# A convolution in transformed blocks: blocks of 4 rows by 2 columns in place of 4 rows, for images 1 to 3

## The chip, the cores and the metric

The kernel runs on one core of a Trainium2 chip. The metric is the time of one execution on the device in microseconds, as the median of several runs. Before the change it is 2772.66 us (three runs, 2771.19 to 2774.41). The core's engines are TensorE (PE), VectorE (DVE), ScalarE (ACT) and GpSimd (POOL); SyncE (SP) issues most DMAs. Each engine takes its instructions in the order in which the program gives them.

## The reference

Four images x of 256 channels and 48 x 48 pixels, all in fp32. Two layers, each added to its input:

```python
x = x + _L0_conv_ref(_gn(x), ...)   # layer 0: 3x3 convolution, batch norm, relu, qkv, attention, projection
x = x + _L1_conv_ref(_gn(x), ...)   # layer 1: dynamic filters, 1x1 convolution, batch norm over the batch

def _L0_conv_ref(Vx, ...):
    x = lax.conv_general_dilated(Vx, conv_w, window_strides=(1, 1), padding='SAME', ...)  # 256 -> 256, 3x3
    x = relu(batch_norm(x + conv_b))          # stored mean and variance
    qkv = einsum('oc,bchw->bohw', qkv_w, x) + qkv_b        # 8 heads of 32
    attn = softmax(einsum('bhdn,bhdm->bhnm', q, k) * scale)
    out = einsum('oc,bchw->bohw', proj_w, einsum('bhem,bhnm->bhen', v, attn)) + proj_b

def _L1_conv_ref(x, W_cat, W_scale, ...):
    guidance = _conv(x, W_cat, pad=1)         # 45 maps: 9 weights for each of 5 dilations
    outs = [x]
    for i, d in enumerate((1, 6, 12, 24, 36)):
        w = softmax(guidance[:, 9 * i:9 * (i + 1)], axis=1)
        outs.append(_dyn_branch(x, w, d))     # 9 shifted copies of x, weighted per pixel
    y = _conv(concatenate(outs), W_scale, pad=0)           # 1x1, then batch norm
```

`_gn` is a group norm with 32 groups. The change concerns the 3x3 convolution of layer 0 alone.

## The kernel before

The 256 channels stand as two halves (`h`) of 128 partitions. An image's 2304 pixels are handled in 6 chunks of 384 (`CH`). The order of all instructions is fixed when the program is built: the kernel keeps a table of estimated engine times (`clock`), and its planner `drive` gives PE the next step that is due by it.

The stages follow each other as start, attention 0, filters 0, attention 1, filters 1, attention 2, filters 2, attention 3, filters 3 with the end. The start stage makes the convolution of image 0 and its qkv alone. The filter stage of image b (`dynamic_filters`, layer 1 of image b) has the convolution and qkv of image b + 1 as filler (`other`): where no step of the filters is due, `drive` takes the next step of the filler. The last filter stage has no such filler.

A filter stage begins with the last projection (`pp`, L1120), the group norm of layer 1 (`pm_n` L662, `pv_n` L672, then the normalisation of `pad` at L636 and L1661) and the guidance product `pg` (L1197) of the first chunks. `far` gathers the dilated filters (matmuls L1395), `near` the filter of dilation 1 (products on DVE at L1461, sums on POOL at L1466), and `mixes` the final 1x1 product `py` (L1561).

The convolution (`conv`) transforms rows only: four output rows come from six input rows (`d`), through six row points `i` in the order `ORDER = (1, 2, 3, 4, 0, 5)`. `inputs` forms the six transformed inputs `v[i]` in three steps, on ACT and on DVE for image 0, on ACT and POOL for the others. For each point, each of two groups of rows `g` and each output half `o`, PE multiplies with six weight tiles (two channel halves by three columns `kx`) of 288 columns into one PSUM tile:

```python
pc = psum_tile(f"pc_{b}_{i}_{g}_{o}")
for h in range(NH):
    for kx in range(3):
        nc.tensor.matmul(m, u[:, h, kx, o * P : (o + 1) * P],
                         halves[g][:, h, i, :, kx : kx + WW], ...)
```

The tiles come from a pool of two buffers (`ps_c`). `outputs` reads each: points 1 and 3 are copied by ACT (`m`, L843), points 2 and 4 give sums and differences on DVE (L846 to L851), points 0 and 5 close four rows of the result (L827, L832, L856) and a relu on ACT (L814) writes `hid`. Then qkv follows: `pq` (L930) for q and k and `pv` (L951) for v. `hid` uses the same buffer as attention's output `ao`.

The transformed weights `u` are made once, in the start stage, by `Made`, and stored to DRAM as `u_d` (L762), six tiles of 768 KB. The filter stages load them back, one tile per row point (`taken`, L725), into a pool of two buffers. In the start stage POOL also issues the loads of all weights, twelve small stores (L1824), the mask copies (L596, L601), and the loads of the other images for their statistics (`xst`, L1692; DVE reads them at L650).

Of the kernel before, what the change touches and what calls it, by code (L numbers as in the profile page):

```python
# [16 lines left out]
N = HH * WW  # L17
# [40 lines left out]
def conv_preact_kernel(  # L58
# [483 lines left out]
    u_d = tc.dram_tile([6, P, NH, 3, C], F32, name="u_d")  # L542
# [3 lines left out]
    with tc.tile_pool(name="w", bufs=1) as wpool, tc.tile_pool(  # L546
        name="act", bufs=1
    ) as act, tc.tile_pool(name="u", bufs=2) as upool, tc.manual_schedule():
# [12 lines left out]
        wqkv = wpool.tile([P, NH, 3, C], F32, tag="wqkv", name="wqkv")  # L561
        wp = wpool.tile([P, NH, C], F32, tag="wp", name="wp")
# [53 lines left out]
        bn_s6 = wpool.tile([P, NH], F32, tag="bn_s6", name="bn_s6")  # L616


        pads = []
        for j in range(2):  # L620
            t = act.tile([P, NH, PADW * PADW], F32, tag=f"pad{j}", name=f"pad{j}")
            t = t.rearrange("p h (r w) -> p h r w", w=PADW)
            nc.gpsimd.memset(t[:, :, 0, :], 0.0)
            nc.gpsimd.memset(t[:, :, PADW - 1, :], 0.0)
            nc.gpsimd.memset(t[:, :, 1 : PADW - 1, 0], 0.0)
            nc.gpsimd.memset(t[:, :, 1 : PADW - 1, PADW - 1], 0.0)
            pads.append(t)
# [94 lines left out]
        def taken(i):  # L722

            u = upool.tile([P, NH, 3, C], F32, tag="u", name=f"u_{i}")
            nc.sync.dma_start(out=u, in_=u_d[i])  # L725
            return u

        class Made:


            def __init__(self, wc, pool):
                self.w = [wc[:, :, 3 * j : 3 * j + 3, :] for j in range(3)]
                self.u = {}
                self.pool = pool

# [10 lines left out]
            def home(self, i):  # L746
                return upool.tile([P, NH, 3, C], F32, tag="u", name=f"u_{i}")
# [4 lines left out]
            def __call__(self, i):  # L752
# [9 lines left out]
                nc.sync.dma_start(out=u_d[i], in_=u[i])  # L762
# [149 lines left out]

        def conv_qkv(b, gn, psum_tile, weights, ready, pool, between=()):

            hid = keep("h", f"hid_{b}")
            yield from conv(b, gn, psum_tile, weights, ready, pool, hid, between)
# [6 lines left out]
            for c in range(NCK):  # L923
                cols = slice(c * CH, (c + 1) * CH)
                for g in range(NH):
                    for s, dst, bias in ((0, q, Q_B), (1, k_, K_B)):
# [18 lines left out]
                        )  # L945
                        yield 2 * MM
# [31 lines left out]
        def attention(b, q, k_, vT, pools, spare, project, scratch):  # L978
# [132 lines left out]
            weigh(*steps[-1], prev)  # L1111
            close(last)
            return ao, chunk
# [25 lines left out]
        def dynamic_filters(b, ao, chunk, norm, other, pools):  # L1139
# [485 lines left out]
            def drive(streams):  # L1625

                due = [next(s, None) for s in streams]
                while any(d is not None for d in due):
# [9 lines left out]
                    else:  # L1638
                        got = next(other, None)
                        if got is not None:  # L1640
                            spent[0] += got
                        elif soonest < NEVER:
                            clock.t["PE"] = soonest

            if alone:
                other = late()

# [144 lines left out]
        u_next = None  # L1792
        norms = {}
# [269 lines left out]
```

## Time and profile before

| | |
|---|---|
| median of three runs | 2772.66 us |
| the profiled execution: time, span | 2766.55 us, 2764.8 us |
| mean granted TensorE clock | 0.99 |
| busy: PE, DVE, ACT, POOL | 95%, 73%, 64%, 23% |
| start stage | 0 to 147.9 us |
| filter stages 0, 1, 2 | 304.2, 303.8, 278.1 us long |
| attention stages | 365 to 370 us each |

How to read it: a line of the profile names the source line, the engine, the operation, output and inputs by the program's names, and the shapes. An fp32 matmul of the program appears as two records on PE. "Idle before" is the time in which the engine did nothing before the instruction, and behind the arrow stands what released it. Times within the trace count from the start of the span.

### The profile page before, as it was taken

To read this page: it belongs to the slowest core of one execution; us is meant where nothing else is said; L and a number is where in the kernel's file an instruction comes from. 1 tells how busy PE (TensorE), PEld (TensorE's weight loads), DVE (VectorE), ACT (ScalarE), POOL (GpSimd) and SP (SyncE) were. 2 spreads that over 40 slices of the span, in tenths; PEclk is the share of its full clock that TensorE was granted. 3 is DMA by queue.
4 is the path that set the end of the run, shared out by engine and by line. 5 is a ranking of instruction groups with operands and counts; after the bars stand their busy time and mean duration, and the time that the engine had idled before them with its cause. 6 is when DMAs were issued, how large, how long until landed. Compare 5 with 4: busy or idle time off the path is not lost. (4 is left out here: it accounts for less than half of the span.)

```text
span 2764.8 us, 42248 instructions
## 1 busy us (share of the span) xinstructions
PE 2638.8 (95%) x17108; PEld 1135.8 (41%) x17108; DVE 2025.3 (73%) x1956; ACT 1761.1 (64%) x2153; POOL 632.3 (23%) x583
## 2 busy tenths in 40 slices
PE   7999999899999999989999999999999999999994
PEld 5632223455662222345565222245566222234452
DVE  6578888656539888856644988894664988885476
ACT  3488988633349888843336889882335988873244
POOL 5100100435400100054430001006542001000352
PEclk9999999999999999999999999999999999999997
DMA  5604544223422444423360345442335244432465
GB/s 216 156 24 103 109 98 104 58 77 90 104 56 58 101 102 97 109 57 75 84 132 9 81 98 112 101 87 56 93 92 150 55 96 95 101 87 68 118 181 182
DMA packets 132522, 267.35 MB, mean 97 GB/s; under 512 B 55656, under 2 KB 97552, under 8 KB 131424
## 3 DMA queue, kind: packets, MB, share of 16 engines
q0 software_dynamic: 25952, 135.74, 21.6%
q1 hardware_dynamic: 106368, 128.84, 17.7%
q8 instruction: 136, 2.23, 0.3%
q14 instruction: 66, 0.54, 0.1%
HBM read 107.40 MB, written 34.46 MB: 51 GB/s over the span
## 5 line engine op out<-in xcount | busy, mean ns | idle before, releaser
L1050 DVE TENSOR_TENSOR acc<-acc,p 128x2048 f32<-128x2048 f32 (+1 forms) x572 | 1061.1, 1855 | 115.6 <-ACT p L1014 64.9
L1014 ACT ACTIVATE p<-se 128x1536 f32<-128x1536 f32 x648 | 938.7, 1449 | 0.1
L1005 PE MATMUL so<-q,k 32*128 32x512 f32 (+1 forms) x1440 | 726.4, 592 | 13.5 <-ACT p L1013 12.7
L1005 PE MATMUL se<-q,k 32*128 32x512 f32 (+1 forms) x4320 | 735.1, 592 | 0.0
L1034 PE MATMUL num<-p,vT 128*32 128x512 f32 (+1 forms) x5760 | 705.1, 560 | 4.6 <-ACT p L1014 2.4
L1013 ACT ACTIVATE p<-so 128x512 f32<-128x512 f32 x648 | 388.4, 599 | 186.8 <-PE se L1005 80.0
L1466 POOL TENSOR_TENSOR near<-near,prod 128x768 f32<-128x768 f32 x192 | 348.8, 1817 | 431.4 <-DVE prod L1461 424.7
L1005 PEld LDWEIGHTS so<-q,k 32*128 32x128 f32 x1440 | 216.1, 183 | 529.0 <-ACT p L1013 489.8
L1034 PEld LDWEIGHTS num<-p,vT 128*32 128x32 f32 x5760 | 133.8, 108 | 478.8 <-issue 444.3
L1054 POOL DMA_DIRECT2D scratch<-p x124 | 105.5, 851 | 772.3 <-ACT p L1014 519.8
L1461 DVE TENSOR_TENSOR prod<-wb,pad 128x768 f32<-128x768 f32 x192 | 181.9, 953 | 87.6 <-ACT wb L1448 75.6
L1561 PE MATMUL py<-far,wsc 128*128 128x384 f32 x704 | 236.7, 488 | 0.0
L1005 PEld LDWEIGHTS se<-q,k 32*128 32x128 f32 x4320 | 226.7, 183 | 5.4 <-ACT p L1014 4.1
L1448 ACT COPY wb<-ws 128x384 f32<-128x384 f32 x216 | 108.7, 507 | 171.3 <-DVE prod L1461 137.6
L1170 ACT COPY far<-far 128x512 f32<-128x512 f32 x82 | 87.9, 1099 | 137.4 <-PE far L1395 134.6
L1052 POOL DMA_DIRECT2D scratch<-p x32 | 17.9, 559 | 669.7 <-ACT p L1014 508.3
L1561 PEld LDWEIGHTS py<-far,wsc 128*128 128x128 f32 x704 | 131.1, 190 | 87.3 <-issue 1.8
L897 PE MATMUL pc<-cv_q,u 128*128 128x288 f32 x576 | 151.8, 415 | 8.2 <-DVE cv_q L788 6.2
L1197 PE MATMUL pg<-pad,wcat 128*45 128x384 f32 x864 | 149.1, 493 | 10.0 <-ACT lg L1255 4.4
L897 PE MATMUL pc<-cv_k,u 128*128 128x288 f32 x576 | 153.3, 410 | 4.3 <-DVE yt L832 2.7
L930 PE MATMUL pq<-hid,wqkv 128*128 128x384 f32 x384 | 125.6, 487 | 1.7 <-DVE yt L832 0.6
L897 PEld LDWEIGHTS pc<-cv_q,u 128*128 128x128 f32 x576 | 108.7, 192 | 43.2 <-DVE cv_q L788 6.3
(252 smaller groups left out, 2368.3 us busy)
## 6 DMA issues: line engine op xcount, KB each, us to landing
scratch<-p POOLq DMA_DIRECT2D x156, 768.0 KB, 5.7
ws<-w_d SPq DMA_DIRECT2D x216, 192.0 KB
pad<-in_x SPq DMA_DIRECT2D x14, 1152.0 KB
u<-u_d SPq DMA_DIRECT2D x18, 768.0 KB
xst<-in_x POOLq DMA_DIRECT2D x36, 192.0 KB, 6.9
x_d<-pad SPq DMA_DIRECT2D x36, 192.0 KB
y_d<-y SPq DMA_DIRECT2D x14, 384.0 KB
u_d<-u SPq DMA_DIRECT2D x6, 768.0 KB
```

The source lines that it names most:

```text
L897: nc.tensor.matmul(m, u[:, h, kx, o * P : (o + 1) * P], halves[g][:, h, i, :, kx : kx + WW], start=(h == 0 and kx == 0), stop=(h == NH - 1 ...
L930: nc.tensor.matmul(pq[:, :CH], wqkv[:, i, s, g * P : (g + 1) * P], hid[:, i, cols], start=(i == 0), stop=(i == NH - 1),)
L1005: nc.tensor.matmul(dst[:, at : at + n], k_[r, g, m * P : (m + 1) * P], q[r, g, q0 : q0 + n], start=True, stop=True,)
L1013: nc.scalar.activation(p[:, 0, :], s1, AF.Exp, scale=QS)
L1014: nc.scalar.activation(p[:, 1:, :], s3, AF.Exp, scale=QS)
L1034: nc.tensor.matmul(st["num"][r, at : at + n], vT[:, m, g * P + j * D : g * P + (j + 1) * D], p[:, j, at : at + n], start=(m == 0 and not s ...
L1050: nc.vector.tensor_tensor(st["acc"][:, js], other[:, js], p[:, js], ALU.add)
L1197: nc.tensor.matmul(pg[64 * s : 64 * s + NG, :CH], wcat[:, ii, k, :], shifted(ii, cc, k // 3 - 1, k % 3 - 1), start=(i == 0 and k == 0), st ...
L1448: nc.scalar.copy(pw[:, :CH], fetched[c, k][0])
L1461: nc.vector.tensor_tensor(prod.rearrange("p h (r w) -> p h r w", w=WW), wb, src, ALU.mult)
L1466: nc.gpsimd.tensor_tensor(cat, cat, prod, ALU.add)
L1561: nc.tensor.matmul(py[c][:, o, :CH], wsc[:, n * NH + i, o * P : (o + 1) * P], rhs, start=(n == 0 and i == 0), stop=(n == order[-1] and i = ...
```

## The change

For images 1 to 3 the convolution is also transformed along the columns: two output columns come from four input columns through four column products. The row transformation stays. Image 0 keeps the old `conv`.

- `Blocks` holds the transformed inputs. `stage0` to `stage3` form the row points from `gn` (1200 elements each), on ACT, DVE and POOL; `stage0` and `stage1` are placed at the end of the attention before, around its last `close`; `stage2` follows the first product of the first tile and `stage3` that of the third. `along(i)` makes the four column inputs of point `i` (576 elements each) on DVE or POOL, into what was v, `hid` or the pad.
- `conv_blocks` makes for each point `i`, each output half `o` and each column product `j` a PSUM tile with two matmuls of 288 columns. Products 1 and 2 are copied by ACT (`one`), summed and subtracted (`both`, `one`) on DVE or POOL, and then joined with products 0 and 3 into the point's output, which goes through the old row sums on 576 elements and a relu.
- The weights are stored in the start stage as column sets (`four`), one per point and output half, 512 KB each, made by ACT and POOL; the filter stages load twelve of them into thirds of one tile `ring`, which replaces the pool of two.
- The filler gives a time from which it can go on (`need`), and `drive` leaves it aside until then.
- Before a pad is loaded again, POOL clears its border (`clear`), as the pad now serves as a buffer.

```diff
-    u_d = tc.dram_tile([6, P, NH, 3, C], F32, name="u_d")
+    u_d = tc.dram_tile([6, NH, P, NH * 4 * P], F32, name="u_d")
...
+        TILES = [(i, o) for i in ORDER for o in range(NH)]
...
+        def taken(t):
+            i, o = TILES[t]
+            at = 1024 * ((t + 2) % 3)
+            u = ring[:, at : at + 1024]
+            nc.sync.dma_start(out=u, in_=u_d[i, o])
+            return u.rearrange("p (h j c) -> p h j c", h=NH, j=4)
...
-                nc.sync.dma_start(out=u_d[i], in_=u[i])
+                for o in range(NH):
+                    four = self.pool.tile([P, NH, 4, P], F32, tag="four", name=f"four_{i}_{o}", bufs=1)
+                    of = u[i][:, :, :, o * P : (o + 1) * P]
+                    nc.scalar.mul(four[:, :, 0], of[:, :, 0], 2.0)
+                    nc.scalar.mul(four[:, :, 3], of[:, :, 2], 2.0)
+                    tt = nc.gpsimd.tensor_tensor
+                    tt(four[:, :, 1], of[:, :, 0], of[:, :, 2], ALU.add)
+                    tt(four[:, :, 2], four[:, :, 1], of[:, :, 1], ALU.subtract)
+                    tt(four[:, :, 1], four[:, :, 1], of[:, :, 1], ALU.add)
+                    nc.sync.dma_start(out=u_d[i, o], in_=four.rearrange("p h j c -> p (h j c)"))
...
+            def stage0(self):
+                v, d = self.v, self.d
+                nc.scalar.mul(v[5], d[1], 4.0)
+                self.axpy(v[0], d[2], -4.0, d[4])
+                nc.gpsimd.tensor_tensor(v[5], d[3], v[5], ALU.subtract)
+            def stage1(self):
+                v = self.v
+                nc.vector.tensor_tensor(v[1], v[0], v[5], ALU.add)
+                self.along(1, nc.vector)
+                nc.gpsimd.tensor_tensor(v[2], v[0], v[5], ALU.subtract)
+            def stage2(self):
+                v, d = self.v, self.d
+                nc.gpsimd.tensor_tensor(v[3], d[4], d[2], ALU.subtract)
+                nc.gpsimd.tensor_tensor(v[6], d[3], d[1], ALU.subtract)
+                self.axpy(v[4], v[6], -2.0, v[3])
+                self.axpy(v[3], v[6], 2.0, v[3])
+            def stage3(self):
+                v, d = self.v, self.d
+                nc.gpsimd.tensor_tensor(v[0], v[0], d[2], ALU.subtract)
+                nc.gpsimd.tensor_tensor(v[5], d[5], v[5], ALU.subtract)
+                self.axpy(v[0], d[0], 4.0, v[0])
+                self.axpy(v[5], d[3], -4.0, v[5])
...
+            blocks.along(2)
+            for t, (i, o) in enumerate(TILES):
+                u = us.pop(t)
+                y = target(i, o).rearrange("p (n s) -> p n s", s=2)
+                parts = []
+                for n, j in enumerate((1, 2, 0, 3)):
+                    m = psum_tile(f"pc_{b}_{i}_{o}_{j}")[:, :XN]
...
+                    for h in range(NH):
+                        nc.tensor.matmul(m, u[:, h, j], z[:, h], start=(h == 0), stop=(h == NH - 1))
+                        clock("PE", MM * XN / CH)
+                        if h == 0:
+                            if n == 0:
+                                if t + 2 < len(TILES):
+                                    us[t + 2] = taken(t + 2)
+                                if o == 0:
+                                    if i == ORDER[0]:
+                                        blocks.stage2()
+                                    elif i == ORDER[1]:
+                                        blocks.along(ORDER[2])
+                                        blocks.stage3()
...
+                    if n < 2:
+                        one = pool.tile([P, XN], F32, tag="one", ..., bufs=4)
+                        nc.scalar.copy(one, m)
+                        parts.append(one)
+                        if n == 1:
+                            both = pool.tile([P, XN], F32, tag="both", ...)
+                            either(both, *parts, ALU.add, end)
+                            either(parts[0], *parts, ALU.subtract, end)
+                            parts[1] = both
...
             weigh(*steps[-1], prev)
+            following[0]()
             close(last)
+            following[1]()
...
-                        got = next(other, None)
-                        if got is not None:
-                            spent[0] += got
-                        elif soonest < NEVER:
-                            clock.t["PE"] = soonest
+                        open_at = need[0]()
+                        if open_at <= clock.t["PE"]:
+                            got = next(other, None)
+                            if got is not None:
+                                spent[0] += got
+                                continue
+                            need[0] = lambda: NEVER
+                        soonest = min(soonest, open_at)
+                        if soonest < NEVER:
+                            clock.t["PE"] = max(soonest, clock.t["PE"])
```

`either` gives an operation to DVE or POOL by the estimated clock; `axpy` is DVE's x * a + y, issued per channel half on the inputs, and not entered in the clock there.

## The prediction

> **What bounds the kernel now.** First the page's busy times, then the windows of each stage, then the timeline at the two places where the change puts new work in front of TensorE.
>
> ```profile
> PE 2638.8 (95%) x17108; PEld 1135.8 (41%) x17108; DVE 2025.3 (73%) x1956; ACT 1761.1 (64%) x2153; POOL 632.3 (23%) x583
> ```
>
> TensorE (PE) is the bound. The windows show where the convolution stands (columns: window, length, busy time and instructions of PE, PEld, DVE, ACT, POOL, granted clock, DMA share, GB/s):
>
> ```profile
> 0.00:147.90 147.90, 126.09 (x491) 93.19 (x491) 88.69 (x186) 57.65 (x100) 49.81 (x148) 1.00 0.57 174
> 513.20:817.40 304.20, 293.85 (x1306) 180.25 (x1306) 161.40 (x238) 109.60 (x185) 123.43 (x76) 0.99 0.33 78
> 1187.80:1491.60 303.80, 293.12 (x1306) 180.05 (x1306) 160.95 (x238) 109.72 (x185) 123.47 (x76) 0.99 0.32 78
> 1857.90:2136.00 278.10, 263.82 (x1211) 161.91 (x1211) 163.69 (x234) 107.06 (x183) 123.75 (x76) 0.99 0.36 97
> ```
>
> The first row is the start stage (convolution of image 0 alone), the others are the three filter stages: dynamic filters of one image, with convolution and qkv of the next as filler. PE is busy for 293 of 304 us there; DVE and POOL have room on average. What their queues do at the beginning of a stage decides this change, so the timeline of the start stage (start, duration, engine, line, what, idle before and its releaser):
>
> ```profile
> 19.65 8.91 PE L897 MATMUL pc<-cv_q,u 128*128 128x288 f32 x24 [6.22 <-DVE cv_q L788]
> 24.07 2.55 POOL L1824 DMA_DIRECT2D w_d<-e  x5 [4.32 <-DMA wsc<-in_scale_w]
> 29.98 6.09 PE L897 MATMUL pc<-cv_k,u 128*128 128x288 f32 x24 [1.41 <-ACT m L843]
> ```
>
> PE starts at 19.65 on ACT's and DVE's input sums; POOL is held by its DMA issues until 26.62; the third block of products waits for ACT's copy `m`. And of the second filter stage:
>
> ```profile
> 1196.26 4.46 PE L1120 MATMUL pp<-ao,wp 128*128 128x384 f32 x8 [2.75 <-DVE ao L1087]
> 1205.42 0.28 PE L662 MATMUL pm_n<-mvn,gmat 128*128 128x2 f32 x2
> 1211.54 2.17 PE L1197 MATMUL pg<-pad,wcat 128*45 128x384 f32 x12 [1.41 <-DVE pad L636]
> ```
>
> The norm's matmul `pm_n` stands in PE's queue at 1205.42, the first guidance product `pg` at 1211.54: everything of the filters comes after these two.
>
> **The sum's base.** The profiled execution took 2766.55 us (span 2764.8); the median of the runs is 2772.66, 6.1 above it. I sum against 2766.55 and add 6.1.
>
> **Products removed.** Per image, 6 row points x 4 blocks x 6 products = 144 become 6 x 2 x 4 x 2 = 96, all of 288 columns. In the start stage, blocks of 12 products (24 records) begin 5.82 us apart (53.84, 59.66, 65.47 on PE's timeline): 0.485 each. 48 x 0.485 = 23.3 us an image, 69.8 for three. As PE is 96% busy there, all of it would count if PE still had work at every moment.
>
> **New weights, start stage.** Each of the 6 weight sets is now turned into four columns twice (`four`, per output half): two ACT multiplications, three POOL adds of 256 elements, one 512 KB store. `four` has one buffer, so the next half's first ACT multiplication waits for the store to land, and in ACT's queue behind it stand the input sums, the `m` copies and the relus. Prices: POOL adds of 600 and 768 elements took 1.45 and 1.82 us, by that line 0.7 for 256, so 2.1 for three; ACT's 288-element copy took 0.40, so 0.7 for two. A store: the 768 KB `u_d` store issued at 50.80 kept the DMA engines busy at 0.93 from 51.6 to 53.7, 2.9 us; scaled, 2.6 for 512 KB. The other end is 5.7 us, the median to landing of the 768 KB `scratch` issue.
>
> - First product: POOL free 26.6, adds 28.7, store 31.4, ACT's second half 32.1, then cv_q multiplication 0.7 and DVE 2.4: PE starts at 35.2 instead of 19.65, +15.5.
> - Third block: DVE's weight sum ends 6.9 after PE's start (as at 26.51 now), 42.1; ACT's `wc` 1.5, two multiplications and POOL's adds together, store: 46.9; second half, table load, `m` copy: 49.7 instead of 29.98, +19.7 in all.
> - Point 3: POOL's mask copies (26.95 to 43.5 now, 16.6 us) follow the adds and end near 65.6. Then three rounds of adds and store (4.8 each) and 1.1 of ACT stand before the `m` copy: 81.1, where PE needs it at 53.84 + 19.7 = 73.5. +27.3 in all.
> - POOL's `xst` loads queue behind `four` adds, and DVE's statistics on them stand before DVE's reads of PSUM: about 3 more (0 to 6).
> - TensorE's clock: new idle times of 5 to 8 us, 2.5 (below).
>
> Sum +33. Bounds: +20 if the mask copies run at the short copies' 0.4 us for three (no wait at point 3) and `xst` costs nothing; +48 with stores of 5.7.
>
> **Start of each filter stage.** The order of the new instructions: POOL forms `v2` before the stage; then `along(2)` writes four 576-element tiles into `hid`, the buffer of `ao`, so it waits for `pp` to be read (about 1201.4, since the input work of stage0 delays DVE's `ao` by 0.6). POOL: 4 x 1.4 = 5.6, then two subtractions of 1200 elements (stage2), 2.75 each by the line of 600 and 768: 1212.5. On DVE, four `axpy` of 600 (0.78 each, as DVE's 600-element sums of image 0) wait for these, and behind them stands the norm's aggregate: 1212.5 + 3.1 + 0.9 = 1216.5. PE's `pm_n`, now at 1205.42, waits until then, +11.2, and the filler products behind it in PE's queue too. Before `pg`, two products of the second tile need ACT copies that stand behind ACT's 2.3 us normalisation: +2 more. On to the first far product (1241 now) I follow the queues to 1261, with 10 more products (4.9 us) done by then: a net stall of 15 us a stage, 45 in all. None of the planner's clocks counts these stage operations, so its order does not avoid it. Bounds: 8 a stage if POOL takes half the time for these, 18 if strided reads slow POOL by a fifth.
>
> **The rest of a filter stage.** DVE's 40 output operations of 288 (18 us) and some copies of far tiles go; about 19 + 4 of 576 (0.72), 24 + 6 of 288 (0.44), 10 of 600 and one of 1200 come: +23 of 161. ACT gains 7 (110 now); POOL's 36 becomes 47. All this lies beside PE. What does not: a column product's PSUM tile lasts 0.97 us instead of 2.9, two buffers, and its copy queues behind 1.1 us far copies on ACT or DVE. After the start, the stage now idles about 2 us; I take 3 more a stage with the clock (0 to 8), 9 in all.
>
> Costed at nothing: `u_d` loads (6.3 MB for 4.7 an image, DMA share 0.32, two tiles ahead; if late, 3 us a tile); clearing pads and their reload (first needed by a projection over 100 us into attention); stage0 and stage1 on DVE before `pp` is read (DVE idles 4.7 there; without that cover 4 us a stage). The filler's yield only changes PE's order.
>
> **Sum.** 2766.55 - 69.8 + 33 + 45 + 9 = 2783.8, and 6.1 more: 2790 us. Measurement can tell about 0.2% (5.5 us) from no change.
>
> **Weighed with the skill.** The row first: after PE's 2.75 us of idle before 1196.26 the clock reads 0.50 in the window 1196.2 to 1199.6, and 1.00 in the next.
>
> ```profile
> 1196.20:1199.60 3.40, 3.34 (x6) 1.85 (x7) 0.00 (x0) 0.00 (x0) 3.25 (x5) 0.50 0.00 0
> ```
>
> The filter stages pay this already; the start stage would pay anew, and 2.5 is one such window and a half at half loss. The Trainium skill, "TensorE: Matmul & The Clock Gate", Part 1, says that the clock halves after an idle window of about 3.4 us and needs as long a busy one to return; by it each longer idle, some six in all, costs 1.7, an estimate of 10 us and a sum of 2797.
>
> For the store, the Trainium skill, "DMA: Bandwidth & Descriptors", Anatomy of one DMA, gives about 2.0 us fixed per DMA plus bytes at 436 GB/s: an estimate of 3.2 us for 512 KB against my 2.6. With some six stores on the path it would make 2794. It speaks against halving stores that are waited for at once.
>
> **Rivals.**
> - PE's saving comes through (faster): the filter stage's start is hidden because POOL's chain is shorter than priced. Place: DVE's `axpy` behind POOL's stage2. It decides once the loss in a stage is under (69.8 - 33 - 5.5) / 3 = 10.4 us. With 4 us a stage: 2772.7 - 69.8 + 33 + 12 = 2748. For: averages of POOL (41%) and DVE (53%) leave room. Against: the queues are in order and PE has no other work there.
> - Balance: the terms cancel, 2767 to 2778; a loss of 10 to 14 a stage.
> - Column hand-over costs more (slower still): each of 48 column tiles waits 0.2 us more, 10 a stage: 2790 + 21 to 30, 2815. For: far copies of 1.1 us on both evacuating engines. Against: PE's order spreads the tiles among filter products.
> - The change doesn't do what it says: no; 96 products stand in the order.
>
> **Chances.** Forecast 0.55 (2778 to 2803), hand-over 0.16, balance 0.12, faster 0.17. Range 2762 to 2815: it takes in the start stage's +20 with 9 a stage and leaves out most of the faster rival and half of hand-over. Faster 0.17, same 0.12, slower 0.71.
>
> **What would show it.** Right: first convolution product near 35 instead of 19.65; start stage 30 us longer; ACT's `four` waiting on the `u_d` store; `pm_n` some 11 us later in each filter stage with DVE's `axpy` waiting for POOL; filter stages of about 298 instead of 304. Wrong: a start stage within 15 us of before, or filter stages under 290.

## The result, and the profile after

The changed kernel takes 2838.76 us (median of four runs, 2834.66 to 2841.35); the kernel before took 2771.93 beside it. The ratio is 1.0239, interval 1.0221 to 1.0257: 67 us slower, where 17 were forecast, and above the top of the range (2815). The profiled execution took 2841.35 us with a span of 2839.6, so it stands 74.8 us above the profiled execution of before (2764.8).

The profile's busy times of the kernel after:

```profile
PE 2605.1 (92%) x16820; PEld 1099.7 (39%) x16820; DVE 2146.8 (76%) x2032; ACT 1784.3 (63%) x2235; POOL 726.8 (26%) x677
```

PE lost 288 records, the 144 products, but only 34 us of busy time, since part of what is left ran at a lower clock; DVE gained 121 us. The windows of the start stage and of the last two filter stages, with the columns as before:

```profile
0.00:188.67 188.67, 133.00 (x491) 96.92 (x491) 92.08 (x187) 65.66 (x124) 77.30 (x184) 0.94 0.46 143
1232.80:1545.95 313.15, 279.58 (x1210) 166.58 (x1210) 202.88 (x265) 115.00 (x206) 142.78 (x93) 0.95 0.33 81
1916.00:2209.00 293.00, 251.38 (x1115) 149.25 (x1114) 198.40 (x255) 111.41 (x200) 151.88 (x99) 0.92 0.30 82
```

The start stage is 40.8 longer (188.7 for 147.9). The filter stages last 311.8, 313.2 and 293.0 for 304.2, 303.8 and 278.1: they were forecast to become 6 shorter and became 8 to 15 longer. In the second, PE idles for 33.6 of 313.15 where it idled for 10.7, and DVE works 202.9 for 161.0. The attention stages and the end differ by 2.2 in all.

The timeline of the start stage shows the three places of the forecast (`m` is ACT's copy of a product's tile):

```profile
31.16 0.42 ACT L780 ACTIVATE four<-ring 128x256 f32<-128x256 f32 x1 [12.63 <-DMA u_d<-four]
35.48 7.76 PE L921 MATMUL pc<-cv_q,ring 128*128 128x288 f32 x24 [22.07 <-DVE cv_q L812]
84.06 6.39 PE L921 MATMUL pc<-cv_k,u 128*128 128x288 f32 x13 [7.43 <-ACT m L867]
```

ACT waits for the store of `four`, the first product starts at 35.48 (forecast 35.2), and point 3 at 84.06 (forecast 81.1). And in the second filter stage:

```profile
1255.87 2.76 POOL L983 TENSOR_TENSOR cv_v<-pad 128x1200 f32<-128x1200 f32 x1
1258.66 2.05 DVE L1000 SCALAR_TENSOR_TENSOR cv_q<-cv_v,cv_k 128x600 f32<-128x600 f32 x2 [7.66 <-POOL cv_v L983]
1262.92 0.59 PE L667 MATMUL pm_n<-mvn,gmat 128*128 128x2 f32 x2 [10.98 <-DVE mvn L664]
1273.64 2.58 PE L1448 MATMUL pg<-pad,wcat 128*45 128x384 f32 x12
```

DVE's `axpy` stands 7.66 us idle for POOL's second subtraction, and PE 10.98 for the norm's aggregate behind it. Counted from the start of the stage, `pm_n` comes at 30.1 instead of 17.6 and `pg` at 40.8 instead of 23.7. The same stage cut at the first and the last sum of `near`, before (two first parts) and after:

```profile
1187.80:1246.90 59.10, 50.88 (x274) 29.25 (x274) 27.21 (x44) 22.75 (x38) 36.23 (x27) 0.97 0.19 53
1246.90:1416.00 169.10, 166.64 (x748) 96.65 (x746) 107.05 (x137) 58.20 (x97) 87.11 (x48) 1.00 0.32 82
```

```profile
1232.80:1318.20 85.40, 59.68 (x282) 35.53 (x283) 50.48 (x71) 21.56 (x41) 46.16 (x33) 0.82 0.21 61
1318.20:1504.00 185.80, 177.95 (x775) 101.79 (x774) 139.89 (x170) 76.86 (x136) 95.88 (x56) 0.99 0.29 78
```

The first part grew by 26.3 us: PE idles in it for 25.7 instead of 8.2, and 15.8 us of its busy time ran at half clock instead of 3.3. The middle part grew by 16.7, with DVE at 75% instead of 63%. More than half of that, 9.5, is work that PE did there and not after it; 5.4 is idle time and 1.8 the clock. The third part, in which the products that the filters left over are made, shrank (75.6 to 42.0). So of what the stage lost to waits and clock, 23.7 us lie in the first part and 7.2 in the middle.

### The profile page after: what moved, and what is told of

The parts are those of the page before. It is cut to its first block, busy times and chain, and to the rows that moved or that the text cites. A ratio compares the mean times of both kernels' runs of the same rounds, so it can differ in the third digit from the quotient of the medians.

```text
span 2839.6 us, 42067 instructions
## 1 busy us (share of the span) xinstructions
PE 2605.1 (92%) x16820; PEld 1099.7 (39%) x16820; DVE 2146.8 (76%) x2032; ACT 1784.3 (63%) x2235; POOL 726.8 (26%) x677
## 3 DMA queue, kind: packets, MB, share of 16 engines
q1 hardware_dynamic: 109824, 135.14, 17.9%
## 5 line engine op out<-in xcount | busy, mean ns | idle before, releaser
L1254 PE MATMUL so<-q,k 32*128 32x512 f32 (+1 forms) x1440 | 726.4, 592 | 16.7 <-ACT p L1262 16.0
L1303 POOL DMA_DIRECT2D ring<-p x124 | 105.5, 851 | 776.0 <-ACT p L1263 481.4
L1301 POOL DMA_DIRECT2D ring<-p x32 | 17.9, 559 | 634.3 <-ACT p L1263 499.5
L1448 PE MATMUL pg<-pad,wcat 128*45 128x384 f32 x864 | 155.3, 509 | 11.0 <-ACT lg L1506 10.0
L1178 PE MATMUL pq<-hid,wqkv 128*128 128x384 f32 x384 | 129.6, 496 | 10.9 <-ACT hid L1050 8.9
L1423 DVE COPY far<-far 128x512 f32<-128x512 f32 x57 | 61.8, 1084 | 59.9 <-PE far L1646 58.6
L1178 PEld LDWEIGHTS pq<-hid,wqkv 128*128 128x128 f32 x384 | 73.7, 194 | 63.6 <-ACT hid L1050 9.9
L1299 DVE TENSOR_TENSOR acc<-p,p 128x2048 f32<-128x2048 f32 x36 | 82.3, 2285 | 19.7 <-ACT p L1263 19.7
```

The source lines that it names most:

```text
L1178: nc.tensor.matmul(pq[:, :CH], wqkv[:, i, s, g * P : (g + 1) * P], hid[:, i, cols], start=(i == 0), stop=(i == NH - 1),)
L1254: nc.tensor.matmul(dst[:, at : at + n], k_[r, g, m * P : (m + 1) * P], q[r, g, q0 : q0 + n], start=True, stop=True,)
L1299: nc.vector.tensor_tensor(st["acc"][:, js], other[:, js], p[:, js], ALU.add)
L1303: nc.gpsimd.dma_start(out=extra, in_=p[:, 1:], accum_op=ALU.add)
L1448: nc.tensor.matmul(pg[64 * s : 64 * s + NG, :CH], wcat[:, ii, k, :], shifted(ii, cc, k // 3 - 1, k % 3 - 1), start=(i == 0 and k == 0), st ...
```

## The experiments

Theory: `four` stands on the start's path; in the filter stages the input sums at the beginning and the column sums in the middle hold up the filters' chain on DVE, so PE's saving comes to nothing. Rivals: TensorE's clock, the weights' loads, too much work on DVE or POOL, an order that does not count the new operations. "Stages" are the start and the three filter stages in us (after: 188.7, 311.8, 313.2, 293.0); "first sum" is the first sum of `near` on POOL, from the start of its stage (59 to 60 before, 84 to 85 after).

**No `four`.**

```diff
-  (two scalar.mul, three gpsimd adds, one store of four)
+  for h in range(NH):
+      nc.sync.dma_start(out=to[:, h, :3], in_=of[:, h])
+      nc.sync.dma_start(out=to[:, h, 3:], in_=of[:, h, 2:])
```

> Leaves out the step that makes four column weights of three (ScalarE's two multiplications and GpSimd's three adds per half): the three raw columns, and the third once more, are stored to u_d straight from the weight sum, so images 1 to 3 get other weights; everything else is the changed kernel. Theory (the wait for a store with one buffer sets the start stage): the start stage falls from 188.7 us to 148 to 152, the time by 37 to 41 to about 2800. Rival (the start stage is longer because GpSimd's adds stand ahead of its xst loads and mask copies, and the stores cost little): the gain would be the same here, but the first product would come only where DVE's sums allow, near 20 us, and the third block of products near 30; if the first product stays near 35 neither holds. Filter stages unchanged at 312, 313 and 293 within 2.

2800.74 us, 1.0107 (1.009 to 1.0124); stages 149.5, 312.9, 313.5, 294.0. All but 1.6 of the start's 40.8 us is `four`; whether by its wait or by POOL's adds this run does not tell, the one with `four` on POOL below does. The filter stages do not move.

**The order of the first input sums.** First, `stage2` ahead of `along(2)`; second, of `stage2` only POOL's subtractions ahead, with its `axpy` at the second tile:

```diff
+            blocks.stage2()
             blocks.along(2)
...
-                                    if i == ORDER[0]:
-                                        blocks.stage2()
```

```diff
+            blocks.stage2()         # the subtractions alone
             blocks.along(2)
...
+                                if t == 1:
+                                    blocks.stage2b()      # the two axpy
```

> GpSimd's two subtractions of stage2 and VectorE's four axpys are issued ahead of along(2), which waits for the projection to be read. Theory (GpSimd's queue order delays the norm): pm_n comes 24 us after the start of a filter stage in place of 30; 6 to 7 us of idle go in each, and with the clock 8 to 9: about 2814. Rival (column hand-over: the loss is spread over the stage): pm_n comes earlier but the stage keeps its length within 3 us, 2830 or more.

> As the run before, and VectorE's four axpys of stage2 wait until the second tile of products, behind the norm's aggregate. Theory: pm_n comes at 19 to 20 us into a filter stage in place of 30 (17.6 in the kernel before); 11 us of idle go and 3 to 5 us of half clock with them, 14 to 16 a stage: about 2796. Rival (column hand-over): under 3 a stage, 2830 or more.

2836.84 us, 1.0246 (1.0228 to 1.0263), and 2836.45 us, 1.0237 (1.022 to 1.0254). `pm_n` came at 29 and at 26.7 instead of 30.1, the first sum at 82 to 85 in both: no gain in time, and the forecasts for `pm_n` (24, and 19 to 20) missed. Why the second moved so little stands in its timeline:

```profile
1244.88 2.74 POOL L982 TENSOR_TENSOR cv_k<-pad 128x1200 f32<-128x1200 f32 x1
1244.91 9.82 DVE L1027 TENSOR_TENSOR cv_v<-cv_k 128x576 f32<-128x576 f32 x4
1247.59 3.27 POOL L983 TENSOR_TENSOR cv_v<-pad 128x1200 f32<-128x1200 f32 x1
```

DVE's four column inputs took 9.82 us beside POOL's subtractions and further POOL sums; in the kernel after the same four took 2.77, beside nothing. Moving a POOL operation away from DVE's wait puts it beside other DVE work, which then stands still.

**The clock.** Products that compute nothing fill PE's waits, 22 ahead of `pm_n` (shown) and ten ahead of the last projection:

```diff
+                if self.tag == "n1" and int(self.name[-1]) < B - 1:
+                    busy(pm, 22)
```

> Adds products that nobody reads: ten of 256 columns ahead of the last projection, 22 ahead of the norm's matmul of the first three images. TensorE is busy in the two long waits of each filter stage, and nothing else moves. Theory (after a wait the granted clock is half for some 13 us, and that costs time of its own): the half clock behind the norm goes, 6 to 8 us a stage, about 2818. Rival (only the idle time itself counts, the half clock is hidden behind other engines): within 5 us of 2839, or slower by what the added products stand in the way.

2841.2 us, 1.0249 (1.0232 to 1.0267); filter stages 312.3, 311.5, 293.3. The stretch at half clock ahead of `pm_n` was gone and nothing was gained in time: there PE waits for DVE's chain, at whatever clock (`pm_n` came at 29.7 in the second stage, for 30.1). Behind `pm_n` half clock came back, for 6.83 us in the second stage and 10.24 in the third. In the first only a window of 3.41 was left; its first sum came 1.4 earlier and the stage was no shorter. What full clock behind `pm_n` would give in the other two, no run shows.

**Later sums, and VectorE alone.** First, `along(2)` and `stage2` in the second tile, and the `axpy` of `stage0` behind the projection (not shown); second, every input and column sum of POOL on DVE; third, both:

```diff
-            blocks.along(2)
...
+                            if t == 1 and n == 2:
+                                blocks.along(2)
+                                blocks.stage2()
```

```diff
-                nc.gpsimd.tensor_tensor(v[3], d[4], d[2], ALU.subtract)
+                nc.vector.tensor_tensor(v[3], d[4], d[2], ALU.subtract)
...
-            if clock.t["POOL"] + 1400 * half <= clock.t["DVE"] + 680 * half:
-                nc.gpsimd.tensor_tensor(out, a, c, op)
```

> VectorE's first axpy pair of stage0 goes behind the projection, and along(2) and stage2 go behind the norm and its normalisation (into the second tile of products). New theory (two-input sums of VectorE and GpSimd's operations hold each other up: along(1) of four took 2.8 us in the changed kernel and 9.8 us beside GpSimd's subtractions in the split run; so moving GpSimd's work out of the norm's way helps only if it does not meet VectorE's sums): pm_n comes at 18 to 20 us into a filter stage in place of 30, the first near sum at 70 to 74 in place of 85, the stage 10 to 14 shorter, about 2800. Rival (whatever is first, the planner's order behind the norm costs the same as before, as it did in the split run): the first near sum stays at 82 or later, 2830 or more.

> All sums of images 1 to 3 on VectorE, in the changed kernel's order; GpSimd keeps only the near sums. Theory (mutual blocking): VectorE's busy time of a filter stage stays near 203 us although it takes over about 47 us of GpSimd's work (about 25 at VectorE's 0.75 us for 576 elements), since its sums no longer wait for GpSimd's; the first near sum comes at 76 to 80 in place of 85 and the stage is 5 to 9 shorter, about 2820. Rival (VectorE is simply overloaded, blocking is small): VectorE rises to 225 or more and the stage grows by 5 or more, 2855.

> Both edits together. Theory (blocking and queue order are two separate losses): 16 to 22 us a stage, about 2782, filter stages near 293. Rival (one of them alone carries the loss): no better than the better of the two by more than 2 us a stage.

2841.28 us, 1.0259 (1.0241 to 1.0277); 2855.37 us, 1.0309 (1.0292 to 1.0326); 2853.13 us, 1.0301 (1.0284 to 1.0318). In the first, `pm_n` came at 19.8, nearly as early as before, and the first sum still at 82 to 84. The wait had moved to the next DVE operation that PE needs:

```profile
1257.90 7.21 DVE L1032 TENSOR_TENSOR hid<-cv_k 128x576 f32<-128x576 f32 x3
1268.72 0.90 PE L1566 MATMUL xa<-ident,own 128*128 128x128 f32 x3 [6.24 <-DVE own L1423]
```

Three column inputs take 7.21 us, while POOL does its two subtractions (1257.62 to 1263.82), and `own` with PE's `xa` stand behind them. With the sums on DVE alone the three filter stages are 12.7 us shorter in all (313.2, 309.0, 283.1), but DVE works longer (209.6 for 202.9 in the second), the first sum comes at 93 to 95, and the attention behind the last of them takes 391.0 for 367.4: the end of the filters runs into it, and PE waits there up to 8.4 us for ACT, and ACT 11.0 for the store of `far`. So taking POOL's help away gains in the stages and loses more behind them.

**GpSimd in the start stage.** The two multiplications and the store of `four` on POOL, so that ACT waits for neither, and the loads of `xst` on SP:

```diff
-                    nc.scalar.mul(four[:, :, 0], of[:, :, 0], 2.0)
-                    nc.scalar.mul(four[:, :, 3], of[:, :, 2], 2.0)
+                    for j, k in ((0, 0), (3, 2)):
+                        nc.gpsimd.tensor_scalar(four[:, :, j], of[:, :, k], 2.0, None, ALU.mult)
...
-                    nc.sync.dma_start(out=u_d[i, o], in_=...)
+                    nc.gpsimd.dma_start(out=u_d[i, o], in_=...)
```

> Start stage only: the two multiplications of four go from ScalarE to GpSimd, the u_d stores are issued by GpSimd behind its own adds, and the xst loads by SyncE. Nothing of image 0 then waits for a store. Theory (ScalarE's wait for the one buffer's store is what moved TensorE): first product near 20 us in place of 35, the start stage 150 to 160 in place of 189, about 2805. Rival (GpSimd's adds block VectorE's sums of image 0 instead): the start stage stays over 170, 2820 or more.

2804.61 us, 1.0118 (1.0101 to 1.0135); start stage 150.6. Its timeline's first product:

```profile
20.69 8.69 PE L921 MATMUL pc<-cv_q,ring 128*128 128x288 f32 x24 [6.68 <-DVE cv_q L812]
```

The same `four` costs 2.7 us instead of 40.8 when ACT's queue does not wait for its store. POOL still does all its adds, and the multiplications besides, so its adds were not the cost. The loads of `xst` moved too, which was not tried by itself.

**Column sums out of PSUM.** The second product is not copied; DVE reads it where it stands:

```diff
-                        nc.scalar.copy(one, m)      # for n == 1
-                            either(both, *parts, ALU.add, end)
-                            either(parts[0], *parts, ALU.subtract, end)
+                        tt(both, m, parts[0], ALU.add)
+                        tt(parts[0], parts[0], m, ALU.subtract)
```

> The sum and the difference of the first two column products are made by VectorE with the second product read straight from PSUM, in place of a copy by ScalarE and two sums of two SBUF tiles on VectorE or GpSimd. Theory (only sums with both inputs in SBUF are held up by GpSimd: 1.96 us in place of 0.46): these sums take 0.45 each whatever GpSimd does; 2 to 4 us a filter stage, about 2830. Rival (column hand-over: a PSUM tile is now held by two operations of 0.45 and by VectorE's queue in place of one copy of 0.4): 3 to 6 us a stage slower, 2850.

2880.46 us, 1.0395 (1.0378 to 1.0412): 42 us worse; filter stages 324.9, 323.8, 302.6. PE's waits in the second (us in total, times, longest):

```profile
PE pc L1101 <- DVE one L1123: 13.9, 4, 10.6
PE pw L1502 <- DVE e L1498: 4.6, 2, 4.2
```

The rival's direction held, above its price (10 to 13 us a stage for 3 to 6). But the longest wait in the first row, 10.6, is not new: it ends 31 us into the stage, where PE waits 11.0 for `pm_n` in the kernel after. What is new lies after the first sum: PE idles 13.8 us there instead of 7.9, and 11.0 us of its busy time ran at half clock instead of 3.7, by waits for `one`, `e` and others. That tiles held in DVE's queue delay these is likely, and not shown.

**Inputs on GpSimd, counted.** With the PSUM sums of above: `along(1)` and `along(2)` on POOL, the subtractions of `stage2` moved to `stage1`, its `axpy` and those of `stage3` one point later, the `axpy` of `stage0` in `stage1`, all entered in the clock. The second kernel has the start stage of above too:

```diff
-                self.along(1, nc.vector)
+                self.along(1, nc.gpsimd)
                 nc.gpsimd.tensor_tensor(v[2], v[0], v[5], ALU.subtract)
+                nc.gpsimd.tensor_tensor(v[3], d[4], d[2], ALU.subtract)
+                nc.gpsimd.tensor_tensor(v[6], d[3], d[1], ALU.subtract)
+                self.subs = clock("POOL", 8200)
...
-            blocks.along(2)
+            blocks.along(2, nc.gpsimd)
```

> The sums of the run before; and in the first 60 us of a filter stage VectorE's queue is kept for the norm and the filters: along(1), along(2) and the subtractions of stages 1 to 3 on GpSimd and ahead of what waits for the projection, VectorE's axpys of stage2 behind the first softmax's input, those of stage3 later, all counted on the planner's clocks. Theory (what is late in a filter stage is VectorE's chain norm, own copy, softmax, amat, and any conv sum that VectorE takes before them or that meets GpSimd's): pm_n at 18 to 20 us, the first guidance product at 24 to 28, the first near sum at 62 to 70 in place of 85; stages 290 to 298, about 2790. Rival (GpSimd's sums are too slow to feed TensorE, the products come late and pile up behind the filters): first near sum early, but the stage over 305, 2825 or more.

> The kernel of the run before with the start stage of e8. Theory (the two losses are independent): 34 to 38 us under the run before, 2752 to 2760, faster than the kernel before the change. Rival: under 30 less.

2823.09 us, 1.0181 (1.0164 to 1.0198), and 2787.66 us, 1.0061 (1.0044 to 1.0078); filter stages of the second 307.2, 304.8, 282.2, first sum at 73 to 75. The new start stage is worth 35 us here, as it was in the kernel after: the two losses are independent. Against the kernel with the same start stage (313.6, 313.3, 291.7) the inputs' order and the PSUM sums together were worth 17 us in time and 6 to 10 a stage; against the PSUM sums alone the order was worth 57. Single stages scatter: the first kernel, with the same code in them, has 303.2, 311.6 and 281.5. What is left shows in the second's timeline:

```profile
1209.47 2.76 POOL L981 TENSOR_TENSOR cv_k<-pad 128x1200 f32<-128x1200 f32 x1
1212.16 5.32 DVE L641 TENSOR_SCALAR pad<-pad,gmean_n,grstd_n 128x2304 f32<-128x2304 f32 x1
```

The normalisation takes 5.32 us, begun just as POOL went from one subtraction to the next; in the kernel after its four took 1.48.

**No late inputs.** Only point 1 keeps its input sums:

```diff
+                if i != 1:
+                    self.end.update({(i, j): 0.0 for j in range(4)})
+                    return
```

> Leaves out the input sums of row points 2, 3, 4, 0 and 5 of images 1 to 3 (stage2, stage3 and their along): all products read the first row point's columns, and the batch norm's scale is a hundredth of what it should be, to keep the numbers small. Weights, products, output sums and planner as in the changed kernel. Theory (the input sums on VectorE and GpSimd in the first 80 us are the loss): pm_n at 19 to 21 us, first near sum at 60 to 64, stages 285 to 291 in place of 312, 312, 293 (the last 268 to 274), about 2770. Rival (column hand-over through two PSUM tiles, or the output sums): stages over 300, 2805 or more.

2879.96 us, 1.0391 (1.0374 to 1.0408); filter stages 326.4, 323.9, 299.6, though the first sum came at 73.5 to 76. Both theories missed: with less work in the stage it is 7 to 15 us longer. Up to the first sum of the second stage PE idles 16.5 us instead of 25.7, but from there to the last sum 19.7 instead of 7.9. PE's waits in the stage:

```profile
PE pc L1101 <- POOL cv_v L1030: 9.6, 3, 5.2
PE pc L1101 <- ACT one L1119: 5.0, 2, 2.9
PE wT L1593 <- DMA wq<-w_d: 3.6, 1, 3.6
```

PE waits in the middle of the stage, for the column products' sums and copies and for the filters. Likely the planner, with no input to wait for, takes the products at other times, and their sums stand in DVE's, POOL's and ACT's queues among the filters' own; this was not tried by itself. The work of the input sums alone is not the loss.

**Earlier subtractions, and pacing.** On the 2787.66 kernel: the two subtractions in `stage0`; the same with a filler step at most every 2 us of the clock; the same again with PSUM sums in the first two tiles only. And pacing alone on the kernel after:

```diff
+                nc.gpsimd.tensor_tensor(v[3], d[4], d[2], ALU.subtract)     # in stage0
+                nc.gpsimd.tensor_tensor(v[6], d[3], d[1], ALU.subtract)
```

```diff
-                        open_at = need[0]()
+                        open_at = max(need[0](), paced[0])
...
+                                if not alone:
+                                    paced[0] += 2000.0
```

> The kernel of e11 with GpSimd's two subtractions for stage2 moved ahead of the last attention sums' close (into stage0), where VectorE has nothing to do with two SBUF inputs for most of the time. In e11 the norm's normalisation took 5.3 us on VectorE beside them, in place of 1.5. Theory (mutual blocking): normalisation 1.5 to 2.7, the first guidance product at 24 to 25 us in place of 27, 2 to 4 us a stage, about 2779. Rival (the blocking is hidden behind other waits): within 3 us of e11's 2788.

> As the run before, and the planner may take a convolution product in the filter phase only every 2.0 us of its clock. Theory (convolution sums that the planner lets in ahead of amat and of the first near sums delay the filters): first near sum at 63 to 68 us in place of 74, stages 5 to 8 shorter, about 2760. Rival (TensorE lacks work when the products are held back, and they pile up behind the filters): same or up to 20 slower.

> As e14, but from the third tile on ScalarE copies both first column products again, as in the changed kernel (e9 read the second from PSUM and lost 42 us). Theory (a PSUM tile that waits in VectorE's queue holds up TensorE): 10 to 25 us under e14, about 2745. Rival (blocked sums of two SBUF tiles cost as much as the held tile): within 5 of e14.

> The changed kernel with nothing but the planner's pacing of convolution products (one every 2.0 us of its clock in the filter phase). Theory: nothing changes up to the norm (pm_n at 30 us), the first near sum comes at 76 to 80 in place of 85, stages 4 to 8 shorter, about 2822. Rival (what is late in the first 80 us comes from the work ahead of the filter phase alone): first near sum within 2 us of 85, 2835 or more.

2800.02 us, 1.0105 (1.0088 to 1.0122); 2809.07, 1.0152 (1.0131 to 1.0172); 2800.45, 1.0118 (1.0099 to 1.0138); pacing alone 2895.77, 1.0462 (1.0444 to 1.0479). Early subtractions made the first sum later (77 to 79). Pacing brought it to 69 to 70, with copies to 67.5, and the filter stages (313.3, 312.7, 290.2, with copies 310.6, 307.5, 283.9) stayed above the 307.2, 304.8, 282.2 of the kernel they start from; with pacing alone the first sum came at 79 and the filter stages took 331.5, 331.7, 302.5. Held-back products pile up and end the stage: with pacing alone 65 us follow the last sum of the second stage instead of 42. In these runs an earlier first sum did not make a stage shorter.

**Late subtractions.** On the 2787.66 kernel, the two subtractions after `along(2)`, clear of the normalisation; then the same with copies from the third tile on and a pace of 1.6 us:

```diff
             blocks.along(2, nc.gpsimd)
+            blocks.stage1b()        # the two subtractions, out of stage1
```

> The kernel of e11 with GpSimd's two subtractions for stage2 moved behind along(2), so that they start only when the norm's normalisation is over. In e11 that normalisation took 5.3 us on VectorE and the shift before it 2.0, in place of 1.5 and 0.2; ahead of along(1) (e13) the subtractions delayed the first products and pm_n by 5. Theory (mutual blocking costs time where VectorE's chain is the path): normalisation 1.5 to 3, pm_n still at 17 to 18, the first guidance product at 24 to 25.5 in place of 27, stages 2 to 4 shorter, about 2778. Rival (the wait only moves on): first near sum at 74 as before, 2785 or more.

> As e17, with ScalarE's copies of both first column products from the third tile on, and a convolution product at most every 1.6 us of the planner's clock in the filter phase. Theory (e14 to e15 gained 9 us by the copies, e13 to e14 brought the first near sum 9 us forward): stages 296 to 302, about 2772, level with the kernel before the change. Rival (products held back pile up behind the filters, 4 us of idle there as in e15): 2780 or more.

2784.08 us, 1.0057 (1.0036 to 1.0078), and 2791.37, 1.0082 (1.0068 to 1.0096). In the first the normalisation fell to a median of 1.89 us and the first sum came at 70 to 74; the gain on 2787.66 is within the scatter (eight runs, 2779 to 2805). Its filter stages are 307.3, 303.9 and 279.9:

```profile
1191.95:1495.85 303.90, 279.31 (x1210) 164.45 (x1210) 200.30 (x273) 108.56 (x190) 139.28 (x87) 0.97 0.34 83
```

PE works 13.8 us less than in this stage before (293.12) and idles 13.9 more (24.6 for 10.7): the whole saving is taken back. This is the lowest time of any form of the change, 54.7 us under the kernel after, and still slower than the kernel before; no form tried is faster than that one. Not tried: this form with ACT's copies and no pacing.

## Why the prediction was right in direction and short in size

By the profiled executions, 17.2 us were forecast (-69.8 + 33 + 45 + 9) and 74.8 measured, 57.5 more. What failed above all are the two terms of the filter stages, 54 us forecast and 97 measured: the stall at the beginning, priced by durations as they are with nothing beside, and DVE's and POOL's new work behind it, taken to lie beside PE.

- **Products removed: 69.8 forecast.** PE's work at full clock fell by 21.2, 21.6 and 22.5 a stage, 65.3 in all, for 23.3 each: 4.5 short. That "all of it would count if PE still had work at every moment" was the condition, and PE did not: its idle time in a filter stage rose by 23 to 27 us.
- **Start: 33 forecast, 40.8 measured**, 7.8 short. Mechanism and places were right: the first product at 35.48 for 35.2, the third block at 50.27 for 49.7, point 3 at 84.06 for 81.1. The store took 2.7 us from its issue (28.48) to ACT's release (31.16), for 2.6. The estimate of 3.2 from the Trainium skill, "DMA: Bandwidth & Descriptors", Anatomy of one DMA, is for the path that GpSimd issues, and SyncE issued these stores; issued by POOL, in the run with `four` there, they took 3.0 us at least and 3.4 in the median. The clock term was low: 14.9 us of busy time at half clock cost about 7.5, not 2.5. The runs without `four` (149.5) and with it off ACT's queue (150.6) show that all but 2 to 3 us of the term go with that wait.
- **Start of each filter stage: 15 a stage forecast, 22 to 24 measured.** One term of it had been costed at nothing, `stage0` ahead of `pp`:

```profile
1235.92 4.43 POOL L970 TENSOR_TENSOR cv_q<-pad,cv_q 128x1200 f32<-128x1200 f32 x1 [12.62 <-ACT cv_q L968]
1237.89 3.79 DVE L1000 SCALAR_TENSOR_TENSOR cv_q<-pad 128x600 f32<-128x600 f32 x2
1244.27 4.28 PE L1371 MATMUL pp<-ao,wp 128*128 128x384 f32 x8 [5.18 <-DVE ao L1336]
```

Two `axpy`, 0.78 each by the forecast's price, took 3.79 beside POOL's subtraction, and `pp` came 2.4, 3.0 and 1.9 us later in the three stages, where 0.6 was allowed. That `pm_n` fits even so (+12.5 for +11.2) is in part luck, since POOL's four sums took 4.5 for 5.6. The mechanism is right as far as that, with PE's wait behind DVE's aggregate, and DVE's behind POOL. Then the gap grew: `pg` +17.1 (forecast +13.2), the first far product +26.3 (forecast +20), and only 2.6 to 3 us more of PE's work, not 4.9, was done by then. The first sum came 24.5, 26.3 and 25.2 us later, and 22 to 24 of them were lost: 23 more than forecast in three stages. Of the loss in a stage some 17 us is idle time and 5 half clock, which the forecast had in the next term.
- **The rest of a stage: 9 forecast in all, about 29 measured** (7, 7 and 15). The term "+23 of 161" for DVE measured +42 (202.9), and "all this lies beside PE" did not hold. This is the step that was wrong as a step and not in size alone: DVE was counted as an engine with room, where it carries the filters' own chain. PE's two longest waits from the first to the last sum of the second stage (us in total, times, longest), and part of DVE's queue ahead of one of them:

```profile
PE xa L1566 <- DVE own L1423: 4.2, 2, 2.1
PE pg L1448 <- ACT lg L1506: 2.4, 1, 2.4
```

```profile
1377.39 1.96 DVE L1032 TENSOR_TENSOR one<-one,one 128x288 f32<-128x288 f32 x1
1381.02 2.25 DVE L1032 TENSOR_TENSOR cv_v<-cv_v,cv_k 128x576 f32<-128x576 f32 x1
1383.98 0.50 DVE L1423 COPY own<-pad 128x384 f32<-128x384 f32 x1
```

In the last of the three stages another wait comes to it: 8.9 of the 16.4 us that PE idles between the first and the last sum pass before `pq`, for ACT's relu behind the last column and row sums. The rival of the column hand-over named the loss, with the tile's copy as its cause and 10 a stage as its price. The size is near, the cause is another: PE's waits for the copies `one` come to 2.2 us in the second stage, one wait, ahead of the first sum.
- **Attention stages and end: nothing forecast, 2.2 measured.**

Of the other terms costed at nothing, the one for the weights' loads held: among PE's waits in the second stage none is on `ring`. The trigger "filter stages under 290" did not fire, nor did a start within 15 us of before.

The faster rival fell for the reason given against it: averages say nothing of the beginning of a stage. Still its premise was not absurd: with the start stage mended, the inputs re-ordered and the column sums read out of PSUM the change comes to 0.6% above before, so some 55 of the 67 us lie in where `four` and the sums stand, and not in the transform: 34 in the start stage, most of the rest in the order of the inputs with the PSUM sums, which were not parted. How the last 12 divide is open. In the profiled executions of that best form and of before the spans differ by 17.9: 2.7 in the start, 5.0 in the three filter stages, 9.5 in the four attention stages, where the attention's own code is the same (between the kernels they scatter from 365 to 376, the two with all sums on DVE apart), 0.7 in the end.

## What to carry to other kernels

Saved products are time only where PE is the last to come: ask of each stage which chain on the other engines it waits for, and put new work behind that chain, not ahead of it; then look what waits there, since in the runs above the wait moved on with the work. An operation that waits for a store or for another engine is priced by what is queued behind it; `four` cost 40.8 us with ACT's queue behind its store, and 2.7 on POOL's queue with the loads of `xst` on SP. Before work is split over DVE and POOL "because both have room", look for long POOL operations beside DVE operations on SBUF, and price those at the time of both.

## What the runs showed of the hardware

DVE and POOL block each other, in the kernel before too, and no step of the prediction allowed for it. Rows by tile (duration in ns, minimum, median, maximum); the first three of the kernel after, the fourth of before:

```profile
L1032 DVE TENSOR_TENSOR one<-one,one x31: 443/458/1961, 585.1 to 2133.2; 128x288 f32<-128x288 f32 x31
L1032 DVE TENSOR_TENSOR cv_k<-cv_k,one x8: 1984/2072/2075, 763.6 to 2136.0; 128x288 f32<-128x288 f32 x8
L1142 DVE TENSOR_TENSOR cv_q<-one,pc x4: 435/454/455, 606.7 to 2152.7; 128x288 f32<-128x288 f32 x4
```

```profile
L856 DVE TENSOR_TENSOR cs<-cs x16: 457/457/1951, 73.2 to 2072.8; 128x288 f32<-128x288 f32 x16
```

The same 288 elements take 0.46 or about 2 us. Two lines of the timeline after say when:

```profile
763.50 1.90 POOL L1717 TENSOR_TENSOR near<-near,prod 128x768 f32<-128x768 f32 x1 [0.90 <-DVE prod L1712]
763.64 2.07 DVE L1032 TENSOR_TENSOR cv_k<-cv_k,one 128x288 f32<-128x288 f32 x1
```

DVE's sum began 0.14 us after POOL's and ended 0.31 after POOL's end (765.40): it stood for the whole of it. With one operand in PSUM (`cv_q<-one,pc`, or `prod` at 0.95 us beside `near`) no such time is seen. The Trainium skill, "SBUF — State Buffer", Who interferes with whom, has this rule: a DVE instruction with two inputs in SBUF contends with a GpSimd instruction that reads SBUF, and one in a two-port mode does too; the later one stands still. The rows above agree, and the normalisation (one input in SBUF: 1.48 against 5.32 us) with the second part, though its rows do not show which came later.

Taken over the second filter stage, DVE's operations stand 32.5 us above what they would take if each had the shortest time of its shape in the trace, against 10.9 in the kernel before; the 21.6 between them are about what the forecast's +23 lacks to the measured +42. The largest parts are the column sums `cv_k<-cv_k,one`, `one<-one,one` and `cv_q<-cv_q,one`. With all sums on DVE it is 17.7. How much of the time of a stage this blocking costs, no run shows by itself: each run that moved it moved the order of the queues too.

The clock fell in shorter idle times than the rule that the prediction weighed. In the second filter stage it halved 2.1 us into an idle time of 10.98 us, for 13.65 us (1254.05 to 1267.70), and windows of 3.41 us came with idle times of 2.42 and 2.16 us. Others of 2.08 to 2.14 had none, nor had one of 2.37 in the kernel before, so the length of the idle time alone does not decide it here. Whether half clock costs depends on whether PE is waited for: filling the longest wait with empty products gained no time.
